# Seven half products for the last outputs of a feed-forward, with a division and a root moved

## The chip, the cores and the metric

The kernel runs on one core of a Trainium2 chip. The time is that of the device for one execution, in microseconds (us), as the median of several runs. The core has five engines that work at once, each through its own queue in order: TensorE (PE: matmuls; PEld: its weight loads), VectorE (DVE), ScalarE (ACT), GpSimd (POOL) and SyncE (SP, which here only issues transfers). SBUF is the working memory, PSUM the memory of eight banks into which TensorE writes.

## The reference

A transformer block with a condition, in float32. x is 4 x 1024 tokens of 512 features; the condition t gives a scale g and an offset b for each norm.

```python
def _tc_rmsnorm(x, t, gw, gb, bw, bb):
    g = (t @ gw.T + gb)[:, None, :]
    b = (t @ bw.T + bb)[:, None, :]
    inv_rms = jax.lax.rsqrt(jnp.mean(x * x, axis=-1, keepdims=True) + EPS)
    return g * x * inv_rms + b

def _attention(x, Wq, Wk, Wv, Wo):          # 16 heads of 32
    attn = jnp.einsum('blhd,bmhd->bhlm', q, k) / scale
    p = jax.nn.softmax(attn, axis=-1)
    o = jnp.einsum('bhlm,bmhd->blhd', p, v).reshape(B, L, D)
    return o @ Wo.T

def _swiglu(x, gate_w, hid_w, out_w):       # 2048 hidden
    return jax.nn.silu(x @ gate_w.T) * (x @ hid_w.T) @ out_w.T

x1 = x + _attention(_tc_rmsnorm(x, t, g1w, g1b, b1w, b1b), Wq, Wk, Wv, Wo)
y = x1 + _swiglu(_tc_rmsnorm(x1, t, g2w, g2b, b2w, b2b), gate_w, hid_w, out_w)
return x + y
```

## The kernel before

Features lie on the 128 partitions, tokens along the rows; the 4096 tokens are 8 blocks of 512 (n). The order of the work on TensorE, VectorE, ScalarE and GpSimd is the order of the program; transfers on SP are placed by the framework.

**The attention** runs in 256 steps g. A step makes the scores of 4 heads for 256 keys and 256 queries (`scores`, four PSUM banks with the tag sc), copies them to SBUF on ScalarE (`keep`, L323), and keeps a running maximum on VectorE (L328, L331). Four steps are one unit j (4 heads, 256 queries), and kind = g % 4 is a step's place in it. Later steps transpose the maximum (mt, L337), reduce it (L343), split it into three bf16 parts (L345 to L348), transpose these (`parts_T`: pt, L353, at the start of kind 1), spread them over the partitions (sp), copy that to shift (L364), add it to the scores (`shifted`, L369), take the exponential (L372) and multiply with v (`weighted`: av, L382). The sum of the exponentials is built by accumulating transfers that GpSimd issues (L396), folded (L404) and summed by TensorE (sum, L414). `inverse` (L422) and `normalize` (L431) are the division of the softmax on VectorE. A block of tokens is 32 steps.

**The feed-forward** of earlier blocks fills TensorE from step 60 (FS) on: two steps work on one pair p = (g - 60) // 2, that is 128 hidden features for 512 tokens, gate and hid together. Their four products of quarters are made as seven half products (Strassen's scheme in Winograd's form) on sums of weights and tokens that are made ahead; in PSUM they are bank a (gate) and bank b (hid): `pair_15`, `take_5`, `add_15`, `pair_26`, `copy_156`, `pair_7`, `sub_5`, `pair_3`, `pair_4`; then `gate_tanh`, `gate` and `hidden` give the tile h[p]. Four pairs later `filler` multiplies a group of four hidden tiles with out_w (`contract`, q = p - 4, into a bank named pc), in four passes of 512 columns, and `take_contract` (L583) adds it to the residual res, which empties the bank. Banks with the tag w are two; a pair's bank a, pc, pt, sp and sum all take them. ow is loaded one contraction ahead.

In an even step with feed-forward VectorE does, in this order: the add of shift, reduction and parts (kind 0), the running maximum, the take of pc, `sub_5`, and then in kind 0 or 2 the division. `in_first` chooses: kind 0 in steps 0, 4, 8, 16 and 20 of each 32, kind 2 in steps 14, 26 and 30.

**The second norm** of blocks 0 to 6 is spread over the steps: squares on ScalarE, mean over the features by TensorE, a copy (`norm_mean`, L157), a transfer of one row to DRAM and back as 128x4 (`compact`, `take`: "few"), `root` (L173, ScalarE's Sqrt with eps as bias), `invert` (L177, VectorE), `put` (SP, to DRAM), `norm_spread` (SP, back to all partitions as totf), `norm_scale` (L199). For block 0 root and invert stand after step e+20, put e+21, spread e+22; for the others e+20, e+21, e+22, e+24. The exponentials and tanh of ScalarE share a table of functions, Sqrt has another.

**After the attention** (from pair 104 to pair 127) only feed-forward is left: each pair's `filler` is split into two halves between the products. After pair 127 the last four contractions stand alone. The scores' banks are not used there.

Of the kernel before, what the change touches and what calls it, by code (L numbers as in the profile page):

```python
# [9 lines left out]

F32 = mybir.dt.float32
BF16 = mybir.dt.bfloat16
AF = mybir.ActivationFunctionType
ALU = mybir.AluOpType
# [10 lines left out]
def tile_cond_transformer_block(  # L25
# [125 lines left out]
    def norm_mean(tag: str, inside: bool):  # L151
        if inside:
            pm = ps_av.tile([P, NB], F32, tag="av", name=f"pm{tag}")
        else:
            pm = ps.tile([P, NB], F32, tag="w", name=f"pm{tag}")
        mm(pm, ones_mean, state[tag], True, True)
        nc.scalar.copy(state[tag], pm)  # L157

    def compact(tag: str, t, rows: int, n: int):

# [3 lines left out]
    def take(tag: str):  # L164

        src = inv_s.pop(tag)
        few = sb.tile([P, src.shape[0] * src.shape[1] // P], F32, tag="few", name=f"few{tag}", bufs=2)
        nc.sync.dma_start(out=few, in_=src.rearrange("h (p c) -> (h p) c", c=few.shape[1]))
        state["few", tag] = few

    def root(tag: str):
        few = state["few", tag]
        nc.scalar.activation(few, few, AF.Sqrt, bias=eps)  # L173

    def invert(tag: str):
        few = state["few", tag]
        nc.vector.reciprocal(few, few)  # L177

    def put(tag: str):
        few = state.pop(("few", tag))  # L180
# [225 lines left out]
    def take_av(j: int):  # L406
        avs[j] = sb.tile([P, HQ], F32, tag="avs", name=f"avs{j}", bufs=2)
        nc.scalar.copy(avs[j], av.pop(j))
# [176 lines left out]
            nc.sync.dma_start(out=out[n][:, d, :], in_=r)  # L585


    NR = NBLK * C * (NB // HQ) * UN
    GB = C * (NB // HQ)
    BS = GB * UN  # L590
# [15 lines left out]
    def after(g, fn, *a):  # L606
        ended.setdefault(g, []).append((fn, a))
# [40 lines left out]
    for n in range(NBLK):  # L648
        g0 = (n + 1) * BS
        pin(g0 + 6, load_res, n)  # L650
        e = g0 if n == 0 else g0 - 4
        go = e + 13 if n < NBLK - 1 else g0 + 8
        for d in range(C):
            first.append((go, None, project_out, (n, d)))
            pin(go - 3 + (d // 2 * 4 if n else 0), load_wo, n, d)
        if n < NBLK - 1:
            tag = f"f{n}"
            after(e + 16, add_res, n)
            for k in range(2):
# [44 lines left out]
    with tc.manual_schedule(  # L704
# [37 lines left out]
        g = 0  # L742
        END = NR + 12
        NP_ = NBLK * NF

        def filler(p: int, tail: bool = False):

# [8 lines left out]
            if q + 1 < NP_:  # L756
                load_ow(q + 1)
            half = FG // 2
            return (
# [14 lines left out]
        while g < END:  # L774
# [40 lines left out]
                keep(g)  # L815
            if kind == 1 and s_on:
                take_av(j_s)
            due = bool(first) and first[0][0] <= g
            if not ffn:
                if x_on:  # L820
# [24 lines left out]
            elif even:  # L845
# [22 lines left out]
            else:  # L868
# [60 lines left out]
        p0 = (END - FS) // 2  # L929
        for p in range(p0, NP_):  # L930
# [81 lines left out]
```

## Time and profile before

| | |
|---|---|
| median of 3 runs | 2449.82 us (2447.05 to 2451.08) |
| the profiled execution | 2455.29 us, of it span 2453.4 us |
| granted clock of TensorE | 0.994 |
| pc (L112), 4096 matmuls of 512 columns | 470.5 us busy |
| L422 RECIPROCAL 128x256, 64 times | 111.6 us, 1744 ns each |
| L583 take of pc, 128 times | 88.2 us, 689 ns each |
| L353 pt, 128 matmuls | 17.6 us |
| ACT_TABLE_LOAD: L372 13, L173 7, L149 5 and single ones | 1283 ns each |
| L396 accumulations issued by GpSimd, 192 | 165.3 us, 9.3 us to landing |
| ow loads, 128 of 256 KB | 3.1 us to landing |

A matmul in float32 is two instructions and each tile of weights is four of 32 columns, so one pass of 128x128 weights over 256 tokens is 8 rows of the trace. A row's duration reaches beyond the start of the next one; how long TensorE takes is read from start to start. A line of the program can be that of a helper: L112 is `mm`, and the tile's name (pa, pb, pc) tells which product it is.

### The profile page before, as it was taken

To read this page: it belongs to the slowest core of one execution; us is meant where nothing else is said; L and a number is where in the kernel's file an instruction comes from. 1 tells how busy PE (TensorE), PEld (TensorE's weight loads), DVE (VectorE), ACT (ScalarE), POOL (GpSimd) and SP (SyncE) were. 2 spreads that over 40 slices of the span, in tenths; PEclk is the share of its full clock that TensorE was granted. 3 is DMA by queue.
4 is the path that set the end of the run, shared out by engine and by line. 5 is a ranking of instruction groups with operands and counts; after the bars stand their busy time and mean duration, and the time that the engine had idled before them with its cause. 6 is when DMAs were issued, how large, how long until landed. Compare 5 with 4: busy or idle time off the path is not lost. (4 is left out here: it accounts for less than half of the span.)

```text
span 2453.4 us, 72677 instructions
## 1 busy us (share of the span) xinstructions
PE 2385.5 (97%) x32553; PEld 1135.9 (46%) x32553; DVE 1940.7 (79%) x2183; ACT 1413.2 (58%) x1495; POOL 172.4 (7%) x207
## 2 busy tenths in 40 slices
PE   8999999999999999999999999999999999999999
PEld 3333334344444544544454544454445445444444
DVE  2688888878799988998899979997999799843332
ACT  3677776765566656665566656665666566512110
POOL 0000000000000000000000000000000000000000
PEclk9999999999999999999999999999999999999999
DMA  6599999988788788889888888898788888853442
GB/s 216 166 304 259 256 258 240 231 202 219 198 205 210 188 226 209 208 207 229 204 200 213 225 197 209 204 230 207 198 207 203 224 200 204 198 165 117 140 131 70
DMA packets 185988, 501.79 MB, mean 205 GB/s; under 512 B 21319, under 2 KB 78663, under 8 KB 158286
## 3 DMA queue, kind: packets, MB, share of 16 engines
q0 software_dynamic: 28656, 208.68, 43.9%
q1 hardware_dynamic: 156734, 288.47, 35.4%
q8 instruction: 256, 4.19, 0.7%
q14 instruction: 54, 0.44, 0.1%
q10 hardware_dynamic: 288, 0.01, 0.0%
HBM read 246.44 MB, written 41.97 MB: 118 GB/s over the span
## 5 line engine op out<-in xcount | busy, mean ns | idle before, releaser
L369 DVE TENSOR_TENSOR raw<-raw,shift 128x2048 f32<-128x2048 f32 (+1 forms) x320 | 588.8, 1857 | 25.6 <-ACT shift L364 25.6
L323 ACT COPY raw<-sc 128x2048 f32<-128x2048 f32 x256 | 479.7, 1874 | 187.4 <-PE sc L316 130.8
L372 ACT ACTIVATE raw<-raw 128x2048 f32<-128x2048 f32 x256 | 490.8, 1917 | 157.1 <-DVE raw L369 154.8
L328 DVE TENSOR_TENSOR rmax<-rmax,raw 128x1024 f32<-128x1024 f32 x384 | 469.5, 1223 | 48.8 <-ACT raw L323 42.2
L112 PE MATMUL pc<-h,ow 128*32 128x512 f32 x4096 | 470.5, 596 | 5.2 <-DMA ow<-in_out_w 4.2
L382 PE MATMUL av<-raw,v 128*32 128x256 f32 x4096 | 271.9, 383 | 35.6 <-ACT raw L372 35.1
L396 POOL DMA_DIRECT2D raw<-raw x192 | 165.3, 861 | 1967.4 <-ACT raw L372 878.9
L316 PE MATMUL sc<-q,k 32*128 32x256 f32 x4096 | 293.3, 400 | 1.0 <-ACT raw L323 1.0
L112 PE MATMUL pa<-x,fa 128*32 128x256 f32 x4096 | 272.5, 384 | 4.1 <-DVE pa L530 4.1
L112 PE MATMUL pa<-sums,fw 128*32 128x256 f32 x4096 | 271.5, 383 | 0.0
L112 PEld LDWEIGHTS pc<-h,ow 128*32 128x32 f32 x4096 | 128.6, 110 | 250.7 <-issue 231.9
L316 PEld LDWEIGHTS sc<-q,k 32*128 32x128 f32 x4096 | 184.9, 184 | 117.4 <-issue 75.8
L112 PE MATMUL pkq<-y,wkq 128*32 128x512 f32 (+1 forms) x1664 | 232.5, 594 | 4.3 <-ACT y L202 4.1
L112 PEld LDWEIGHTS pa<-x,fa 128*32 128x32 f32 x4096 | 124.7, 110 | 119.7 <-DVE pa L530 21.4
L382 PEld LDWEIGHTS av<-raw,v 128*32 128x32 f32 x4096 | 110.4, 109 | 149.4 <-ACT raw L372 66.0
L112 PEld LDWEIGHTS pa<-sums,fw 128*32 128x32 f32 x4096 | 134.4, 111 | 90.0 <-issue 3.4
L583 DVE SCALAR_TENSOR_TENSOR res<-pc,res 128x512 f32<-128x512 f32 x128 | 88.2, 689 | 78.9 <-PE pc L112 76.2
L545 ACT COPY pb<-pa 128x256 f32<-128x256 f32 x128 | 46.1, 360 | 174.4 <-PE pa L112 173.3
L562 ACT ACTIVATE t<-pa 128x512 f32<-128x512 f32 x128 | 78.1, 610 | 109.9 <-PE pa L112 109.6
L112 PE MATMUL pb<-x,fw 128*32 128x256 f32 x2048 | 134.0, 379 | 1.2 <-ACT pb L545 1.2
L112 PE MATMUL pa<-x,fw 128*32 128x256 f32 x2048 | 134.0, 379 | 0.0
L552 DVE TENSOR_TENSOR pb<-pb,p 128x256 f32<-128x256 f32 x128 | 55.0, 430 | 99.8 <-PE pb L112 94.2
(108 smaller groups left out, 2243.7 us busy)
## 6 DMA issues: line engine op xcount, KB each, us to landing
raw<-raw POOLq DMA_DIRECT2D x192, 1024.0 KB, 9.3
fw<-sw SPq DMA_DIRECT2D x128, 512.0 KB, 7.8
fa<-in_gh_w SPq DMA_DIRECT2D x128, 384.0 KB, 6.8
ow<-in_out_w SPq DMA_DIRECT2D x128, 256.0 KB, 3.1
wkq<-in_kq_w SPq DMA_DIRECT2D x32, 512.0 KB, 6.2
v<-vs SPq DMA_DIRECT2D x128, 128.0 KB, 6.6
k<-kqs SPq DMA_DIRECT2D x124, 128.0 KB, 6.5
kqs<-st SPq DMA_DIRECT2D x61, 256.0 KB, 8.3
```

Source lines behind the costliest of these rows:

```text
L112: nc.tensor.matmul(dst[k : k + n, :], w[:, k : k + n], moving, start=start, stop=stop, skip_group_check=seeded)
L316: nc.tensor.matmul(sc[:, i, k, :], keys[rows, k * P : (k + 1) * P], queries[rows, :], start=True, stop=True)
L323: nc.scalar.copy(raw[r].rearrange("p k h q -> p h k q"), state.pop(("sc", r)))
L328: nc.vector.tensor_tensor(rmax[j], rmax[j], raw[r][:, k, :, :], ALU.max)
L369: nc.vector.tensor_tensor(t, t, s.unsqueeze(1).to_broadcast(list(t.shape)), ALU.add)
L372: nc.scalar.activation(raw[r], raw[r], AF.Exp)
L382: nc.tensor.matmul(av[j][i * DH : (i + 1) * DH, :], v[m, u][:, k, i * DH : (i + 1) * DH], raw[r][:, k, i, :], start=(kt == 0), stop=(kt == ...
L396: nc.gpsimd.dma_start(out=acc[j].rearrange("p k h q -> p (k h q)"), in_=raw[r].rearrange("p k h q -> p (k h q)"), accum_op=ALU.add,)
L545: nc.scalar.copy(bank_b[p][:, RIGHT], bank_a[p][:, RIGHT])
L552: nc.vector.tensor_tensor(b[:, LEFT], b[:, RIGHT], fifth.pop(p), ALU.subtract)
L562: nc.scalar.activation(state["t", p], bank_a[p], AF.Tanh, scale=0.5)
L583: nc.vector.scalar_tensor_tensor(r, pp, 0.5, r, ALU.mult, ALU.add)
```

## The change

Three parts.

1. **Outputs.** The contractions of pairs 108 to 127 and the four after the last pair are made as seven half products, too, with two outputs d and four hidden tiles together. The sums of out_w are made once and kept (for each group and two outputs, 16 pieces of 128x128 in a tile with the tag raw, free by then), the sums of the hidden tiles once for each group. The products are made in the four scores' banks, two of which a matmul each opens first (as L541 does for bank b). ow is no longer loaded for them.
2. **Division.** In steps with feed-forward `divide` is called ahead of `evict` (the take of pc), no longer after `sub_5`.
3. **Root.** `norm_mean` adds eps in its copy. `root` and `invert` are replaced by `inverse_root`, an integer first guess on VectorE and four Newton steps on GpSimd, after step e+21; put comes at e+22, spread at e+23 for block 0 and e+24 for the others.

```diff
-        nc.scalar.copy(state[tag], pm)
+        nc.scalar.activation(state[tag], pm, AF.Identity, bias=eps)
...
-    def root(tag: str):
+    def inverse_root(tag: str):
         few = state["few", tag]
-        nc.scalar.activation(few, few, AF.Sqrt, bias=eps)
-    def invert(tag: str):
-        few = state["few", tag]
-        nc.vector.reciprocal(few, few)
+        y, t = (sb.tile(list(few.shape), F32, tag=f"few{i}", name=f"few{i}{tag}") for i in range(2))
+        nc.vector.tensor_scalar(
+            y.bitcast(I32), few.bitcast(I32), 1, 0x3FFFFFFF, ALU.logical_shift_right, ALU.bitwise_xor
+        )
+        nc.gpsimd.tensor_scalar_mul(y, y, 1.35 * 2.0**62)
+        for _ in range(4):
+            nc.gpsimd.tensor_tensor(t, y, y, ALU.mult)
+            nc.gpsimd.tensor_tensor(t, t, few, ALU.mult)
+            nc.gpsimd.tensor_scalar(t, t, -0.5, 1.5, ALU.mult, ALU.add)
+            nc.gpsimd.tensor_tensor(y, y, t, ALU.mult)
+        state["few", tag] = y
...
+    def output_sums(f: int, k: int):
+        w = sb.tile([P, 16, P], F32, tag="raw", name=f"wt{f}_{k}", bufs=RAW)
+        for i in range(2):
+            nc.sync.dma_start(out=w[:, 4 * i : 4 * i + 4, :], in_=out_w[f, 2 * k + i])
+    def output_sums_add(f: int, k: int):
+        nc.vector.tensor_tensor(s1, a21, a22, ALU.add)
+        nc.vector.tensor_tensor(s2, s1, a11, ALU.subtract)
+        nc.vector.tensor_tensor(s3, a11, a21, ALU.subtract)
+        nc.vector.tensor_tensor(s4, a12, s2, ALU.subtract)
+    def hidden_sums(gr: int):
+        t = sb.tile([P, 4, 2, HQ], F32, tag="raw", name=f"ht{gr}", bufs=RAW)
+        for i in range(4):
+            for k in range(2):
...
+                nc.vector.tensor_tensor(t[:, i, k], a, b, ALU.subtract)
+    def output_steps(gr: int, k: int):
...
+        def step_1():
+            times(a[:, 0], a11, left(one), True)
+        def step_5():
+            times(a[:, 1], s1, sums_of(0))
+            p5.append(sb.tile([P, HQ], F32, tag="avs", name=f"o5_{gr}_{k}", bufs=2))
+            nc.scalar.copy(p5[0], a[:, 1])
+            nc.vector.tensor_tensor(a[:, 1], a[:, 0], p5[0], ALU.add)
+        def step_26():
+            times(a[:, 0], a12, left(two))
+            times(a[:, 1], s2, sums_of(1))
+            nc.scalar.copy(b[:, 1], a[:, 1])
+        def step_7():
+            times(b[:, 1], s3, sums_of(2))
+            nc.vector.tensor_tensor(b[:, 0], b[:, 1], p5[0], ALU.subtract)
+        def step_3():
+            times(a[:, 1], s4, right(two))
+            take(0, a)
+        def step_4():
+            times(b[:, 0], a22, sums_of(3))
+            take(1, b)
...
-            after(e + 20, root, tag)
-            after(e + (20 if n == 0 else 21), invert, tag)
-            after(e + (21 if n == 0 else 22), put, tag)
-            after(e + (22 if n == 0 else 24), norm_spread, tag)
+            after(e + 21, inverse_root, tag)
+            after(e + 22, put, tag)
+            after(e + (23 if n == 0 else 24), norm_spread, tag)
...
                 if g < NR:
                     running_max(g, 0)
                     running_max(g, 1)
+                divide()
                 if evict is not None:
                     evict()
                 pair_7(p)
                 sub_5(p)
...
-            if n_on and j_n < direct and kind in (0, 2):
-                at = g - kind
-                in_first = j_n % GB == GB - 1 or (at >= FS and at % BS not in (12, 24, 28))
-                if in_first == (kind == 0):
-                    inverse(j_n)
-                    if j_n != GB:
-                        normalize(j_n)
+            if not ffn:
+                divide()
...
+        state["outs"] = ps_sc.tile([P, HG, 2, HQ], F32, tag="sc", name="outs")
+        for i in (1, 3):
+            nc.tensor.matmul(...)        # one each into banks 1 and 3
+        def last_filler(p: int):
+            gr, i = (p - FG) // FG, p % FG
+            if i % 2 == 0:
+                return (lambda: (one(), five())), two_six, (lambda: None)
+            return (lambda: (seventh(), three())), four, (lambda: None)
...
+            if p < p0 + NF // FG:
+                for k in range(2):
+                    output_sums((seven // FG - 1 + p - p0) % (NF // FG), k)
...
-            one, two, evict = filler(p, True)
+            one, two, evict = filler(p, True) if p < seven else last_filler(p)
...
+            if p0 + 1 < p <= p0 + 1 + NF // FG:
+                for k in range(2):
+                    output_sums_add((seven // FG - 1 + p - p0 - 2) % (NF // FG), k)
+            if p % FG == FG - 1 and p >= seven - 1:
+                hidden_sums(p // FG)
-        for p in range(NP_, NP_ + FG):
-            one, two, evict = filler(p)
-            one()
-            two()
-            evict()
+        one, other = (output_steps(NP_ // FG - 1, k) for k in range(2))
+        one[0]()
+        other[0]()
+        for i in range(1, 6):
+            one[i]()
+            other[i]()
```

`take(d, bank)` in `output_steps` adds the bank to res on VectorE, as `take_contract` did, and stores the result after the last group. seven is 108, p0 is 104.

More of the change, by code (lines that the diff above doesn't have):

```diff
@@ L11 @@
 F32 = mybir.dt.float32
+I32 = mybir.dt.int32
 BF16 = mybir.dt.bfloat16
@@ L166, in take @@
         src = inv_s.pop(tag)
-        few = sb.tile([P, src.shape[0] * src.shape[1] // P], F32, tag="few", name=f"few{tag}", bufs=2)
+        few = sb.tile([P, src.shape[0] * src.shape[1] // P], F32, tag="few", name=f"few{tag}")
         nc.sync.dma_start(out=few, in_=src.rearrange("h (p c) -> (h p) c", c=few.shape[1]))
         state["few", tag] = few
-    def root(tag: str):
+    def inverse_root(tag: str):
         few = state["few", tag]
-        nc.scalar.activation(few, few, AF.Sqrt, bias=eps)
-    def invert(tag: str):
-        few = state["few", tag]
-        nc.vector.reciprocal(few, few)
+        y, t = (sb.tile(list(few.shape), F32, tag=f"few{i}", name=f"few{i}{tag}") for i in range(2))
[9 more added lines that the diff above has]
+        state["few", tag] = y
     def put(tag: str):
@@ L585, in take_contract @@
             nc.sync.dma_start(out=out[n][:, d, :], in_=r)
+    def output_sums(f: int, k: int):
+        w = sb.tile([P, 16, P], F32, tag="raw", name=f"wt{f}_{k}", bufs=RAW)
+        for i in range(2):
+            nc.sync.dma_start(out=w[:, 4 * i : 4 * i + 4, :], in_=out_w[f, 2 * k + i])
+        state["wt", f, k] = w
+    def output_sums_add(f: int, k: int):
+        w = state["wt", f, k]
+        a11, a12, a21, a22, s1, s2, s3, s4 = (w[:, i : i + 2, :] for i in range(0, 16, 2))
+        nc.vector.tensor_tensor(s1, a21, a22, ALU.add)
+        nc.vector.tensor_tensor(s2, s1, a11, ALU.subtract)
+        nc.vector.tensor_tensor(s3, a11, a21, ALU.subtract)
+        nc.vector.tensor_tensor(s4, a12, s2, ALU.subtract)
@@ new lines, in hidden_halves @@
+    def hidden_halves(gr: int, i: int):
+        return [h[gr * FG + 2 * i + k] for k in range(2)]
+    def hidden_sums(gr: int):
+        t = sb.tile([P, 4, 2, HQ], F32, tag="raw", name=f"ht{gr}", bufs=RAW)
+        one, two = hidden_halves(gr, 0), hidden_halves(gr, 1)
+        for i in range(4):
+            for k in range(2):
+                b11, b12, b21, b22 = one[k][:, LEFT], one[k][:, RIGHT], two[k][:, LEFT], two[k][:, RIGHT]
+                a, b = ((b12, b11), (b22, t[:, 0, k]), (b22, b12), (b21, t[:, 1, k]))[i]
+                nc.vector.tensor_tensor(t[:, i, k], a, b, ALU.subtract)
+        state["ht", gr] = t
@@ new lines, in output_steps, with times, left, right @@
+    def output_steps(gr: int, k: int):
+        banks = state["outs"]
+        a, b = banks[:, 2 * k], banks[:, 2 * k + 1]
+        w = state["wt", gr % (NF // FG), k]
+        a11, a12, _, a22, s1, s2, s3, s4 = (w[:, i : i + 2, :] for i in range(0, 16, 2))
+        one, two, t = hidden_halves(gr, 0), hidden_halves(gr, 1), state["ht", gr]
+        p5 = []
+        def times(dst, weights, moving, start: bool = False):
+            for i in range(2):
+                mm(dst, weights[:, i, :], moving[i], start and i == 0, i == 1, True)
+        def left(tiles):
+            return [x[:, LEFT] for x in tiles]
+        def right(tiles):
+            return [x[:, RIGHT] for x in tiles]
+        def sums_of(i):
+            return [t[:, i, 0], t[:, i, 1]]
+        def take(d: int, bank):
+            n, d = gr * FG // NF, 2 * k + d
+            r = res[n][:, d, :]
+            nc.vector.scalar_tensor_tensor(r, bank.rearrange("p a q -> p (a q)"), 0.5, r, ALU.mult, ALU.add)
+            if gr % (NF // FG) == NF // FG - 1:
+                nc.sync.dma_start(out=out[n][:, d, :], in_=r)
+        def step_1():
[18 more added lines that the diff above has]
+            take(1, b)
+        return step_1, step_5, step_26, step_7, step_3, step_4
@@ L744, in tile_cond_transformer_block @@
         NP_ = NBLK * NF
+        seven = ((END - FS) // 2 // FG + 1) * FG
         def filler(p: int, tail: bool = False):
@@ L755, in filler @@
                 pp = ps.tile([P, NB], F32, tag="w", name=f"pc{q}")
-            if q + 1 < NP_:
+            if q + 1 < seven - FG:
                 load_ow(q + 1)
@@ L817, in tile_cond_transformer_block, with divide @@
                 take_av(j_s)
+            def divide():
+                if n_on and j_n < direct and kind in (0, 2):
+                    at = g - kind
+                    in_first = j_n % GB == GB - 1 or (at >= FS and at % BS not in (12, 24, 28))
+                    if in_first == (kind == 0):
+                        inverse(j_n)
+                        if j_n != GB:
+                            normalize(j_n)
             due = bool(first) and first[0][0] <= g
@@ L929, in tile_cond_transformer_block @@
         p0 = (END - FS) // 2
+        state["outs"] = ps_sc.tile([P, HG, 2, HQ], F32, tag="sc", name="outs")
+        for i in (1, 3):
+            nc.tensor.matmul(
+                state["outs"][:, i].rearrange("p a q -> p (a q)"),
+                select[:, 0, :],
+                select.rearrange("p h c -> p (h c)"),
+                start=True,
+                stop=True,
+            )
+        steps = {}
+        def last_filler(p: int):
+            gr, i = (p - FG) // FG, p % FG
+            if i % 2 == 0:
+                steps[gr, i // 2] = output_steps(gr, i // 2)
+            one, five, two_six, seventh, three, four = steps[gr, i // 2]
+            if i % 2 == 0:
+                return (lambda: (one(), five())), two_six, (lambda: None)
+            return (lambda: (seventh(), three())), four, (lambda: None)
         for p in range(p0, NP_):
```

## The prediction

> **What bounds the kernel now.** I read the page's first two parts for the engine that sets the time, then the list of waits for what stops it, then the timeline of single steps. The page first (busy time and share; then tenths of each of 40 slices):
>
> ```profile
> PE 2385.5 (97%) x32553; PEld 1135.9 (46%) x32553; DVE 1940.7 (79%) x2183; ACT 1413.2 (58%) x1495; POOL 172.4 (7%) x207
> PE   8999999999999999999999999999999999999999
> ```
>
> TensorE has no idle slice, at a granted clock of 0.994. So a change counts in two ways only: columns that TensorE no longer streams, and waits of TensorE that appear or go. VectorE is at 79% over the span, but 9 tenths in most slices before the last six: while scores run, it is just behind. The change moves a division in its queue, so I looked at a step of kind 0 and the start of the next (kind 1). VectorE (start us, duration us, instruction):
>
> ```profile
> 996.66 1.22 DVE L331 TENSOR_TENSOR rmax<-raw 128x1024 f32<-128x1024 f32 x1
> 998.28 0.69 DVE L583 SCALAR_TENSOR_TENSOR res<-pc,res 128x512 f32<-128x512 f32 x1 [0.41 <-PE pc L112]
> 999.22 0.43 DVE L552 TENSOR_TENSOR pb<-pb,p 128x256 f32<-128x256 f32 x1 [0.24 <-PE pb L112]
> 999.56 1.74 DVE L422 RECIPROCAL total<-total 128x256 f32<-128x256 f32 x1
> 1001.33 0.42 DVE L431 TENSOR_TENSOR oT<-avs,total 128x256 f32<-128x256 f32 x1
> 1001.68 2.35 DVE L369 TENSOR_TENSOR raw<-raw,shift 128x1024 f32<-128x1024 f32 x2
> ```
>
> TensorE over the same stretch:
>
> ```profile
> 993.55 1.09 PE L337 MATMUL mt<-ident,rmax 128*128 128x128 f32 x8
> 994.57 3.64 PE L112 MATMUL pc<-h,ow 128*32 128x512 f32 x32
> 998.03 1.05 PE L112 MATMUL pb<-x,fw 128*32 128x256 f32 x16
> 999.03 0.27 PE L353 MATMUL pt<-ident_bf,split 128*32 128x128 bf16 x2
> 999.23 1.15 PE L316 MATMUL sc<-q,k 32*128 32x256 f32 x16
> ```
>
> The reader is to see one coincidence: L583, which empties the bank of pc, ends at 998.97, and the transpose pt starts at 999.03. It is no accident. pt needs a bank with tag w; there are two, one holds the gate sums of the running pair, the other pc. In the step around 604 the take ran 7 us late behind a weight load, ended at 603.94, and pt started at 603.99. Everything of TensorE after pt stands behind it in its queue. So in every step of kind 0 the take is on the path already.
>
> **The change part by part.**
>
> *Division ahead of the take.* The reciprocal and the product with avs now stand between the maximum (L331) and L583. From the rows: consecutive VectorE instructions overlap by 0.08, so the reciprocal starts at 997.80; the product 1.77 later (999.56 to 1001.33 above), 999.57; the take 0.35 after that (1001.33 to 1001.68), 999.92; it ends at 1000.61, and pt starts 0.06 later, at 1000.67 instead of 999.03: **1.64 us of TensorE idle**. Only the 0.41 that VectorE waited for pc hides any of it. In steps 0 and 16 of a block the take waited 0.10 only, which gives 1.94, but there VectorE had a backlog of 0.3 that a stalled TensorE lets it work off; I take 1.65 throughout. Where: kind 0 steps 0, 4, 8, 16 and 20 of each 32 from step 64 on, 30 of them, and step 256. Step 64 has no outputs yet, at 68 the take is late anyway; at 256 VectorE waits 1.22 for pc, so 0.9 remains. 28 x 1.65 + 0.9 = **+47.1**. Nothing gives it back: what follows pt (copy mT, sp, shift, scores' copy, exponential) all starts from pt, and VectorE only idles longer before L369.
> In the steps of kind 2 (14, 26, 30) no transpose follows. At 14 VectorE's idle 0.12 and 0.24 (951.23, 952.16) are filled, and the two TensorE gaps that end that chain, 0.28 at 958.90 and 0.20 at 960.17, go: 0.48 x 6 = **-2.9**. At 26 and 30 there is no idle to fill. At 26 the next gate sums find the bank 0.35 late (1045.87 against 1046.2), which the gap of 1.57 at 1051.29 absorbs.
>
> *The second root.* It leaves ScalarE, and with it two table loads in each of 7 blocks. The first (966.00) lies in idle time. The second does not; ScalarE, then TensorE:
>
> ```profile
> 973.10 0.39 ACT L408 COPY avs<-av 128x256 f32<-128x256 f32 x1
> 973.51 1.28 ACT L372 ACT_TABLE_LOAD   x1
> 974.80 1.91 ACT L372 ACTIVATE raw<-raw 128x2048 f32<-128x2048 f32 x1
> ```
>
> ```profile
> 974.22 1.15 PE L316 MATMUL sc<-q,k 32*128 32x256 f32 x16
> 976.76 1.07 PE L382 MATMUL av<-raw,v 128*32 128x256 f32 x16 [1.39 <-ACT raw L372]
> ```
>
> ScalarE goes copy, load, exponential without a pause, and TensorE idles 1.39 for the exponential. Without the load it comes 1.28 earlier and 0.11 is left: 7 x 1.28 = **-9.0**. The Trainium skill ("ScalarE: Activation LUTs", What ACT_TABLE_LOAD costs) adds a drain of about 1380 ns to the 1283 ns of the load, some 2.66 us for each switch; by that the sum would be 18.6, capped by the gap at 9.7. The rows show no drain (0.01 on either side), so the row decides. The mean's copy with a bias costs 0.07 more, in idle time.
>
> In its place VectorE runs one shift where the small reciprocal stood (0.17, no change), and GpSimd 17 dependent instructions on 128x4. Queued behind them on GpSimd is the next accumulation, at 983.50, late enough; on SP the store of the result waits for them, and behind it stand a v load, the read-back into totf and the next output weights ow. In the trace the store went at 979.10, the read-back 2.65 later; an ow load lands in 3.1, an issue takes 0.33. The weights are needed by pc at 994.57. So 15.5 - 2.65 - 0.33 - 3.1 = 9.4 us are free for the 17, or 0.55 each. The nearest rows are GpSimd's own at the start, a fill and a dependent select on 128x128 that follow each other by about 0.25: 17 x 0.25 = 4.2 us, no cost. Against this speaks the Trainium skill ("SBUF — State Buffer", Who interferes with whom): a VectorE instruction with two SBUF inputs and a GpSimd instruction that reads SBUF exclude each other, the later one blocking to the end of the first. From 978.99 VectorE runs 4.6 us of such instructions (L369 2.26, L328 twice 1.22) and again from 984.5; if the 17 get in once per such instruction and four times in each pause of about 1 us, they need some 12 us, an estimate: 2.5 late, in 6 blocks (the first has no ow): +15. No row of before has GpSimd computing beside VectorE. I take **0**, as the GpSimd row has it; a gain is excluded, since nothing waits for the root today (totf is used only around 1013). Far end +15.
>
> *Seven half products.* The stage after the attention is TensorE alone. Its busy time there (us in the window, engines in the order of the page), and the last stretch:
>
> ```profile
> 2247.20:2433.40 186.20, 186.20 (x2840) 92.03 (x2836) 58.88 (x101) 26.15 (x59) 0.00 (x0) 1.00 0.40 121
> ```
>
> ```profile
> 2433.34 15.63 PE L112 MATMUL pc<-h,ow 128*32 128x512 f32 x144
> ```
>
> No gap at all. A pair takes 9.48 (its first gate product starts at 2237.77, 2247.25, 2256.72) and streams 7 x 512 + 4 x 512 = 5632 columns: 1.683 ns each, the same for 256-column and 512-column products. Two outputs of one group of hidden tiles cost 4096 columns; as seven half products 3584. 24 contractions (20 beside pairs 108 to 127, 4 after) save 24 x 256 = 6144 columns: **-10.3**. What comes back:
> - two seeding matmuls of the scores' banks, one such (L541) takes 0.39: +0.6 for both, between 0.4 and 0.8;
> - at pair 108 the first product of differences needs the hidden sums, which stand on VectorE behind the take (to 2248.2) and eight weight sums of pair 107. An addition of 128x256 in SBUF takes 0.42 and follows the last by 0.34 (L480 to L483): 8 x 0.34 + 0.43 after 2248.1 is 2251.3, while TensorE wants it at 2247.25 + 1.72 + 0.86 = 2249.8: +1.4. At later groups no weight sums stand ahead and the sums are in time: the take to about 0.8 after the pair's end, the first sum at 1.2, wanted at 2.6;
> - after the last pair eight hidden sums end about 3.4 after it, so that the first bank's addition comes at 3.9 where TensorE wants the bank at 3.4: +0.5. Otherwise one bank's copy and addition (0.37 + 0.43) lie behind the other's product of 0.86;
> - the last four results leave within 2.5 us instead of 10: 0 to +1 for the last store, +0.5.
> Between odd pairs the cover of the fifth product's addition falls from 1.72 to 0.86. It ends at 2245.81, the next pair would start at 2246.4: still hidden, by 0.5. The weight loads of 1 MB a pair for four pairs fit where the DMA share is 0.40. Sum of this part **-7.3**.
>
> **Sum.** 47.1 - 2.9 - 9.0 + 0 - 7.3 = **+27.9**. It is made on the profiled execution, which took 2455.29 (span 2453.4, the rest around it), 5.5 over the median of the three shown; the differences do not depend on that, so 2449.82 + 28 = **2478**. Its own range, with a stall of 1.35 to 1.95 at each take (36 to 55), the tail between -9 and -5 and the root at -7 to -10, is 2465 to 2492.
>
> **Rivals.**
> 1. *The later take costs nothing, because pt gets its bank otherwise or VectorE reaches that point earlier.* Then -2.9 - 9.0 - 7.3 = -19.2, **2431**. For it: VectorE waits 0.41 and 0.24 around the take today, which the division fills. Against: of its 2.1 us only 0.41 lies before the take, and 603.94 to 603.99 shows pt following it. It decides from a stall under 19.2 / 28.5 = 0.67 us a step.
> 2. *Half of it is absorbed.* If VectorE's earlier finish of the division shortens the later waits for the exponential (35.1 us in all for av), 19 to 25 of the 47 stay, and the result is within 5 us of before: **2452**. Against: the long ones (1.57 at 1051.29) arise in steps 26 and 27, after VectorE has waited for TensorE again.
> 3. *GpSimd is locked out*, +15 more: **2493**. For it the skill's rule; against, the small size of the work, which fits into VectorE's new idle time after each take.
>
> **How the numbers follow.** The forecast 0.62, the first rival 0.15, the second 0.11, the third 0.12. A change under 0.2% (5 us) is about what a measurement of this kernel cannot tell from none. The first rival is faster; the second gives 0.03 faster, 0.05 same, 0.03 slower; the others are slower: 0.18, 0.05, 0.77. The range takes in the second and third and leaves out the first: 2446 to 2503.
>
> **What would show it.** Right: in the steps of kind 1 after a division, pt starts 0.06 after the take and 1.6 later against pb than before; the take ends 2.7 after the maximum instead of 1.1; the table loads fall by 14 and the gap of 1.39 to about 0.1; the last stage shortens by 7, with one gap at pair 108. Wrong: steps 1, 5, 9, 17, 21 of a block no longer than before, or pt waiting for something else. GpSimd's 17 instructions lasting over 9 us, with pc waiting for ow two steps later, would be the third rival.

## The result

The changed kernel takes 2547.36 us (median of 4 runs, 2541.72 to 2547.90), the kernel before in the same series 2450.45 (median of 4; a fourth run, of 3478.25 us, stands beside the three shown above and hardly moves the median): **1.0395 times the time before, 95% interval 1.0374 to 1.0416**. That is 97 us more, where 28 had been forecast. The sign was right, the size was not, and the time lies outside the range. The profiled execution took 2547.13 us (span 2545.3).

The page of the changed kernel, its first two parts, then the row of one of its groups, behind it the same row of before (busy time, mean ns | idle time ahead of it and what ended it):

```profile
PE 2402.1 (94%) x33131; PEld 1155.9 (45%) x33131; DVE 1975.2 (78%) x2287; ACT 1402.1 (55%) x1498; POOL 265.9 (10%) x326
...
PE   8999999999989999999999999999999998999997
...
POOL 0000000200020002000210002000200020000000
...
L113 PE MATMUL pb<-x,fw 128*32 128x256 f32 x2048 | 139.1, 391 | 21.6 <-ACT pb L553 21.6
```

```profile
L112 PE MATMUL pb<-x,fw 128*32 128x256 f32 x2048 | 134.0, 379 | 1.2 <-ACT pb L545 1.2
```

TensorE's share falls from 97% to 94%. Of the 92 us by which the span is longer, TensorE stands idle for 75 (143.2 us of the span against 67.9) and is busy for 17 more (2402.1 against 2385.5), though it has fewer columns to stream. The slices of POOL show a new visitor: seven places, one for each of blocks 0 to 6, where GpSimd computes. And pb waits 21.6 us in all for a copy of ScalarE, where it waited 1.2.

**The division did what was forecast.** VectorE, then TensorE, at step 20 of a block of 32 and the start of step 21 (the same stretch of before was shown with the prediction):

```profile
1006.31 1.22 DVE L339 TENSOR_TENSOR rmax<-raw 128x1024 f32<-128x1024 f32 x1
1007.45 1.75 DVE L430 RECIPROCAL total<-total 128x256 f32<-128x256 f32 x1
1009.23 0.42 DVE L439 TENSOR_TENSOR oT<-avs,total 128x256 f32<-128x256 f32 x1
1009.57 0.69 DVE L591 SCALAR_TENSOR_TENSOR res<-pc,res 128x512 f32<-128x512 f32 x1
```

```profile
1007.69 1.05 PE L113 MATMUL pb<-x,fw 128*32 128x256 f32 x16
1010.31 0.27 PE L361 MATMUL pt<-ident_bf,split 128*32 128x128 bf16 x2 [1.57 <-DVE res L591]
```

The take ends at 1010.26, 2.7 after the maximum ended, and pt starts 0.05 later, behind an idle of 1.57. The view of the tile pt counts such waits:

```profile
  DVE res L591: 48.1, 29
```

48.1 us in 29 places, of which the trace of before has none; the sum in the prediction had 47.1, from 28 and a smaller one. They are not all alike: pt waits 1.57 in steps 5, 9 and 21, but 1.88 in steps 1 and 17:

```profile
1111.93 0.27 PE L361 MATMUL pt<-ident_bf,split 128*32 128x128 bf16 x2 [1.89 <-DVE res L591]
```

The prediction had worked out 1.94 for these steps and then put them down to 1.65.

**The rest was not forecast.** GpSimd in the same block (each row: start, duration, instruction, and in brackets the idle time before it):

```profile
988.82 2.18 POOL L179 TENSOR_SCALAR few0f<-few0f 128x4 f32<-128x4 f32 x1 [9.50 <-DVE few0f L176]
...
993.74 0.20 POOL L184 TENSOR_TENSOR few0f<-few0f,few1f 128x4 f32<-128x4 f32 x1
...
994.29 2.21 POOL L182 TENSOR_TENSOR few1f<-few1f,fewf 128x4 f32<-128x4 f32 x1
...
1003.93 0.20 POOL L184 TENSOR_TENSOR few0f<-few0f,few1f 128x4 f32<-128x4 f32 x1
1004.43 0.91 POOL L404 DMA_DIRECT2D raw<-raw  x1 [0.31 <-issue]
```

The chain lasts from 988.82 to 1004.13, 15.3 us, and the accumulation (L404) that stands behind it in GpSimd's queue goes out at 1004.43. Some 20 us later this reaches ScalarE and, through it, TensorE:

```profile
1026.11 1.87 ACT L331 COPY raw<-sc 128x2048 f32<-128x2048 f32 x1 [7.26 <-DMA raw<-raw]
1027.88 0.38 ACT L553 COPY pb<-pa 128x256 f32<-128x256 f32 x1
```

```profile
1028.31 1.94 PE L113 MATMUL pb<-x,fw 128*32 128x256 f32 x16 [3.94 <-ACT pb L553]
1030.17 2.09 PE L324 MATMUL sc<-q,k 32*128 32x256 f32 x16
```

The next accumulation waits for this one's landing and leaves at 1014.60, some 10 us later, and so on. A late one hands back its buffer of the tag raw late; the copy of the scores waits 7.26 for a buffer; behind it in ScalarE's queue is the copy that pb needs; and TensorE stands still for 3.94. After that the same 16 matmuls last 1.94 where they last 1.05 elsewhere, and the scores 2.09 in place of 1.15. The view by windows (busy time of PE, PEld, DVE, ACT and POOL, then the granted clock, DMA share and GB/s) tells why:

```profile
1023.63:1027.04 3.41, 0.74 (x8) 0.00 (x0) 0.00 (x0) 0.93 (x1) 0.50 (x1) 1.00 0.98 372
1027.04:1030.45 3.41, 2.14 (x20) 0.88 (x24) 2.40 (x3) 3.04 (x3) 0.43 (x2) 0.50 0.91 214
1030.45:1033.87 3.42, 3.42 (x32) 1.73 (x36) 3.42 (x6) 1.54 (x1) 0.78 (x1) 0.50 1.05 207
```

TensorE's clock is halved for two windows of 3.41 us. In the profile of before there are 6 such windows between 592 us and the last matmul, in that of the changed kernel 18: eleven with such a wait of pb in steps 22 and 23, four after the division's wait of 1.88 (below), three elsewhere.

**The stage after the attention grew.** From the mean of the last norm (pmf) to the end of the span before takes 239.6 us, in the changed kernel 249.8: 10.2 more, where -7.3 was forecast. Its columns are fewer as counted; but in every odd pair from 109 on, and in nearly every step after the last pair, a product waits:

```profile
2343.51 1.07 PE L113 MATMUL outs<-h,wt 128*32 128x256 f32 x16 [0.62 <-DVE outs L670]
...
2532.48 1.07 PE L113 MATMUL outs<-ht,wt 128*32 128x256 f32 x16 [0.61 <-DVE outs L670]
2534.11 1.07 PE L113 MATMUL outs<-h,wt 128*32 128x256 f32 x16 [0.56 <-DVE outs L670]
2535.99 1.07 PE L113 MATMUL outs<-h,wt 128*32 128x256 f32 x16 [0.81 <-DVE res L650]
```

The first of these writes the right half of bank a. L670, which it waits for, works in bank b.

### The profile page after: what moved, and what is told of

Its sections match the earlier page's. It is cut to its first block, busy times and chain, and to the rows that moved or that the text cites. A ratio compares the mean times of both kernels' runs of the same rounds, so it can differ in the third digit from the quotient of the medians.

```text
span 2545.3 us, 74065 instructions
## 1 busy us (share of the span) xinstructions
PE 2402.1 (94%) x33131; PEld 1155.9 (45%) x33131; DVE 1975.2 (78%) x2287; ACT 1402.1 (55%) x1498; POOL 265.9 (10%) x326
## 5 line engine op out<-in xcount | busy, mean ns | idle before, releaser
L377 DVE TENSOR_TENSOR raw<-raw,shift 128x2048 f32<-128x2048 f32 (+1 forms) x320 | 589.6, 1858 | 95.2 <-ACT shift L372 95.2
L113 PE MATMUL pc<-h,ow 128*32 128x512 f32 x3328 | 381.6, 598 | 2.9 <-DMA ow<-in_out_w 2.0
L404 POOL DMA_DIRECT2D raw<-raw x192 | 165.6, 862 | 1881.1 <-ACT raw L380 753.4
L324 PE MATMUL sc<-q,k 32*128 32x256 f32 x4096 | 301.7, 409 | 1.2 <-ACT raw L331 1.2
L390 PE MATMUL av<-raw,v 128*32 128x256 f32 x4096 | 279.2, 392 | 23.6 <-ACT raw L380 23.1
L113 PE MATMUL pa<-x,fa 128*32 128x256 f32 x4096 | 269.9, 381 | 4.2 <-DVE pa L538 2.5
L113 PE MATMUL pa<-sums,fw 128*32 128x256 f32 x4096 | 267.8, 379 | 0.0
L113 PE MATMUL pkq<-y,wkq 128*32 128x512 f32 (+1 forms) x1664 | 231.2, 593 | 4.3 <-ACT y L210 4.1
L113 PEld LDWEIGHTS pc<-h,ow 128*32 128x32 f32 x3328 | 103.6, 110 | 209.5 <-issue 195.0
L113 PEld LDWEIGHTS pa<-x,fa 128*32 128x32 f32 x4096 | 123.3, 109 | 113.0 <-DVE pa L538 20.4
L113 PEld LDWEIGHTS pa<-sums,fw 128*32 128x32 f32 x4096 | 132.8, 110 | 88.2
L113 PE MATMUL pb<-x,fw 128*32 128x256 f32 x2048 | 139.1, 391 | 21.6 <-ACT pb L553 21.6
L363 ACT COPY mT<-pt 12x256 bf16<-12x256 bf16 x64 | 23.2, 362 | 223.6 <-PE pt L361 223.6
L113 PE MATMUL pa<-x,fw 128*32 128x256 f32 x2048 | 134.3, 380 | 0.0
L113 PE MATMUL pb<-sums,fa 128*32 128x256 f32 x2048 | 133.9, 379 | 0.0
L113 PEld LDWEIGHTS pkq<-y,wkq 128*32 128x32 f32 (+1 forms) x1664 | 72.8, 117 | 127.7 <-issue 116.7
```

The lines of the kernel that those rows point to most:

```text
L113: nc.tensor.matmul(dst[k : k + n, :], w[:, k : k + n], moving, start=start, stop=stop, skip_group_check=seeded)
L324: nc.tensor.matmul(sc[:, i, k, :], keys[rows, k * P : (k + 1) * P], queries[rows, :], start=True, stop=True)
L363: nc.scalar.copy(mT[j][:NP], pt[:NP, :, :].rearrange("p a b -> p (a b)"))
L377: nc.vector.tensor_tensor(t, t, s.unsqueeze(1).to_broadcast(list(t.shape)), ALU.add)
L390: nc.tensor.matmul(av[j][i * DH : (i + 1) * DH, :], v[m, u][:, k, i * DH : (i + 1) * DH], raw[r][:, k, i, :], start=(kt == 0), stop=(kt == ...
L404: nc.gpsimd.dma_start(out=acc[j].rearrange("p k h q -> p (k h q)"), in_=raw[r].rearrange("p k h q -> p (k h q)"), accum_op=ALU.add,)
```

## The experiments

Ten kernels. "Before" is the median of the runs of before beside them (2448.60, 2449.51 and 2450.31 us in three series).

| kernel | median us | ratio to before (95%) | half-clock windows |
|---|---|---|---|
| division alone | 2497.32 | 1.0202 (1.0175 to 1.0230) | 3 |
| root alone | 2485.55 | 1.0150 (1.0132 to 1.0168) | 11 |
| seven half products alone | 2463.81 | 1.0057 (1.0039 to 1.0074) | 3 |
| the same, a tile for each bank | 2447.13 | 0.9991 (0.9983 to 1.0000) | 2 |
| and its weights loaded later | 2445.19 | 0.9983 (0.9976 to 0.9991) | 4 |
| root on VectorE | 2447.55 | 0.9991 (0.9983 to 1.0000) | 3 |
| root on GpSimd in three lots | 2444.78 | 0.9981 (0.9974 to 0.9988) | 2 |
| division, product twice | 2534.76 | 1.0348 (1.0333 to 1.0362) | 19 |
| that, with scores made twice | 2506.37 | 1.0225 (1.0210 to 1.0240) | 0 |
| best of the parts | 2437.36 | 0.9942 (0.9926 to 0.9957) | 3 |

The last column counts windows of 3.41 us at half clock, from 592 us to the last matmul, in the one profiled execution of each. Another execution can have others: of the four of the division alone, one took 2507.72 us at a clock of 0.993, the profiled one 2497.71 at 0.996.

### One part at a time

The first kernel has only this:

```diff
                 if g < NR:
                     running_max(g, 0)
                     running_max(g, 1)
+                divide()
                 if evict is not None:
                     evict()
```

> The kernel before with the division alone moved ahead of the take. Theory: the waits of pt for the take grow by about 50 us as in the changed kernel's trace, and because TensorE then stands idle for 1.6 us in one window of its clock more often, the granted clock falls for some windows of 3.4 us more, worth 5 to 15 us: 2510 us (2500 to 2520). Rival A: the waits are all of it and the clock has other causes: 2494 us. Rival B: the division costs nothing by itself and the changed kernel's loss comes from late accumulations: 2445 to 2453 us.

Measured: +48.7 us, clock 0.996. Rival A is right: the waits are all of it. The tile pt waits `DVE res L583: 48.1, 29` as in the whole change, and only 3 windows are at half clock. My theory had added 5 to 15 us for the clock; where the border lies, the section on the clock shows.

The second has `norm_mean`, `take`, `inverse_root`, `put` and `norm_spread` of the change and nothing else.

> The kernel before with the second root alone moved to GpSimd. Theory: ScalarE's table loads go (-10 us), but the 17 instructions hold GpSimd's queue for 10 to 15 us, the accumulations behind them start late, the scores' copy waits for a raw buffer at step 22 of each block, and TensorE stands idle there 4 us and runs at half clock for some windows after it: 4 to 6 us for each of six blocks, 2450 - 10 + 30 = 2470 us (2460 to 2482). Rival: the late accumulations only show where the division has made the queue late already, and the root alone gains: 2440 us.

Measured: +37 us, somewhat over the upper end, and nothing of the rival. Fourteen table loads are gone, and step 18 of each of seven blocks is 1.41 us shorter, as in the change, where the product with v no longer waits (it waited 1.39 for the exponential before):

```profile
985.30 1.15 PE L324 MATMUL sc<-q,k 32*128 32x256 f32 x16
986.42 1.07 PE L390 MATMUL av<-raw,v 128*32 128x256 f32 x16
```

The chain takes it back several times over. TensorE in this kernel, one block earlier than the rows above:

```profile
746.33 3.62 PE L113 MATMUL pc<-h,ow 128*32 128x512 f32 x32
754.10 1.94 PE L113 MATMUL pb<-x,fw 128*32 128x256 f32 x16 [4.15 <-ACT pb L553]
755.97 1.79 PE L324 MATMUL sc<-q,k 32*128 32x256 f32 x16
```

The same wait and the same half clock behind it, without the division. Against before, steps 21 to 23 are 6.8 to 8.3 us longer in each of the six blocks that have feed-forward there. Together that is 46.4 us; less 7 x 1.41 for the table loads it is 36.5, which is the +37.

The third has the new functions and the loops after the attention alone.

> The kernel before with the seven half products alone, as they are in the change (one tile of four banks). Theory: the columns saved are -10, and the waits of the products for other banks' work in the same tile about +20: 2460 us (2456 to 2464). Rival: these waits come from VectorE's state that the other two parts left behind, and the part alone gains the 7 us forecast: 2443 us.

Measured: +15.2 us. The rival falls: the waits have nothing to do with the other parts. The three parts alone add up to 48.7 + 37.0 + 15.2 = 100.9 us; together they cost 97. So each can be explained by itself, but for a few us: the half-clock windows fall differently in each kernel.

### Whose bank a product waits for

```diff
-    ps_sc = ctx.enter_context(tc.tile_pool(name="ps_sc", bufs=1, space=PSUM))
...
+    sc_pool = tc.tile_pool(name="ps_sc", bufs=1, space=PSUM)
+    ps_sc = sc_pool.__enter__()
...
-        state["outs"] = ps_sc.tile([P, HG, 2, HQ], F32, tag="sc", name="outs")
+        sc_pool.__exit__(None, None, None)
+        ps_out = ctx.enter_context(tc.tile_pool(name="ps_out", bufs=1, space=PSUM))
+        state["outs"] = [ps_out.tile([P, 2, HQ], F32, tag=f"o{i}", name=f"outs{i}") for i in range(HG)]
...
-        a, b = banks[:, 2 * k], banks[:, 2 * k + 1]
+        a, b = banks[2 * k], banks[2 * k + 1]
```

> As the run before, but with four tiles of one bank each in place of one tile of four banks; products, columns and order of the instructions unchanged. Theory (a product waits for the last access to any part of its tile, so separate tiles take away the waits between banks): 2443 us (2439 to 2447). Rival (the products truly need what they wait for): 2460 us, as with one tile.

Measured: 2447.13 us, at the upper edge of the theory and 13 below the rival; and the profile has the theory's picture. From pmf to the end it takes 232.4 us: 7.2 less than before, and 17.5 less than with one tile. Of the waits of odd pairs none is left, of those after the last pair one; TensorE, in the order of time:

```profile
2430.21 1.07 PE L113 MATMUL outs<-h,wt 128*32 128x256 f32 x16 [0.73 <-DVE outs L654]
2431.10 1.05 PE L113 MATMUL outs<-ht,wt 128*32 128x256 f32 x16
```

So products with one tile waited for work in other parts of it. In these two kernels the framework orders by tile, not by bank: the same products, in four banks and in the same order, wait with one tile and do not with four.

The stage is 7.2 us shorter, the whole kernel 1.5. Where did the rest stay? Just ahead of that stage. In this kernel, and then in before, TensorE at the last sum of exponentials:

```profile
2166.91 0.64 PE L415 MATMUL sum<-raw,ones_sum 128*32 128x256 f32 x8 [4.45 <-DVE raw L405]
2168.03 5.11 PE L113 MATMUL pc<-h,ow 128*32 128x512 f32 x32 [0.48 <-ACT total L420]
```

```profile
2171.74 0.64 PE L414 MATMUL sum<-raw,ones_sum 128*32 128x256 f32 x8 [1.64 <-DVE raw L404]
2172.86 3.64 PE L112 MATMUL pc<-h,ow 128*32 128x512 f32 x32 [0.48 <-ACT total L419]
```

The wait is 2.8 longer, and the same 32 matmuls behind it last 5.11 in place of 3.64: half clock again. The queue of SP shows what may be in the way of the last accumulations: `wt`, the 4 MB of weights for the half products, which VectorE first reads at 2235.95:

```profile
2104.10 8.77 SPq L594 DMA_DIRECT2D wt<-in_out_w  x3
...
2148.24 6.57 SPq L594 DMA_DIRECT2D wt<-in_out_w  x6
```

The framework places SP's transfers, and it sent the first of these 132 us ahead of that read. To test whether they are the cause, they were issued by ScalarE, whose order is that of the program:

```diff
-            nc.sync.dma_start(out=w[:, 4 * i : 4 * i + 4, :], in_=out_w[f, 2 * k + i])
+            nc.scalar.dma_start(out=w[:, 4 * i : 4 * i + 4, :], in_=out_w[f, 2 * k + i])
```

> The seven half products with one tile for each bank, and the 16 loads of out_w for them issued by ScalarE at pairs 104 to 107 in place of SyncE, whose queue sent them 100 to 50 us earlier, beside the last accumulations. Theory (these loads delay the last accumulation by 2.8 us, and TensorE's wait for it then costs a half-clock window, 1.7 us): 2443 us (2440 to 2445), and the wait of the last sum is 2.0 us instead of 4.8. Rival (that wait is chance): 2447 us.

Measured: 2445.19 us, just over the theory. Its ratio to before (0.9976 to 0.9991) overlaps that of the four tiles (0.9983 to 1.0000), so that the time alone does not show a gain over them. The rows do: the long wait is gone (`2167.45 0.64 PE L415 MATMUL sum<-raw,ones_sum 128*32 128x256 f32 x8 [0.50 <-PE pa L113]`), but ScalarE's issues now stand ahead of the copy to pb, where TensorE waits 2.05 at 2228.94, in place of 1.20, and a half-clock window follows. Moving the transfers removed one cost and brought another.

### What the root costs on GpSimd

First without GpSimd: the Newton steps as 14 instructions of VectorE.

```diff
-            nc.gpsimd.tensor_tensor(t, y, y, ALU.mult)
-            nc.gpsimd.tensor_tensor(t, t, few, ALU.mult)
-            nc.gpsimd.tensor_scalar(t, t, -0.5, 1.5, ALU.mult, ALU.add)
-            nc.gpsimd.tensor_tensor(y, y, t, ALU.mult)
+            nc.vector.scalar_tensor_tensor(t, y, -0.5, y, ALU.mult, ALU.mult)
+            nc.vector.tensor_tensor(t, t, few, ALU.mult)
+            nc.vector.scalar_tensor_tensor(y, t, 1.5, y, ALU.add, ALU.mult)
```

> The kernel before with the second root alone moved, its Newton steps on VectorE (14 small instructions) in place of GpSimd's 17. Theory (GpSimd's queue is the loss: accumulations behind the chain start late and raw buffers come free late): the loss of the root alone goes, the table loads' 10 us stay gained, VectorE's 14 instructions cost up to 2 us a block: 2444 us (2438 to 2452), and no wait of pb at step 22. Rival (the loss is the later schedule of the root, put and spread): 2480 to 2488 us, as with GpSimd.

Measured: 2447.55 us, within the theory, and pb has no wait in step 22. The loss belongs to GpSimd, not to the root's later place. (Of the 9.9 us won by the table loads 8.4 go back: steps 19 and 20 are 1.4 us longer in six blocks.) The next kernel keeps all 17 on GpSimd, cuts them into three lots with the queue's accumulations in between, and starts them one step earlier:

```diff
-            after(e + 21, inverse_root, tag)
+            after(e + 20, root_start, tag)
+            after(e + 20, root_rounds, tag, 1, False)
+            after(e + 21, root_rounds, tag, 1, False)
+            after(e + 22, root_rounds, tag, 2, True)
```

> The root alone moved to GpSimd as in the change, but the 17 instructions in three lots, behind the accumulations of three steps, the first a step earlier. Same instructions, same neighbours on VectorE. Theory (an accumulation queued behind the whole chain is the loss): an accumulation waits for a third of the chain at most; at least half of the 37 us goes: 2440 to 2465 us. Rival (it is the shared use of SBUF by GpSimd and VectorE, or the root's later end): 2478 to 2490 us.

Measured: 2444.78 us, 4.7 faster than before, where the uncut chain is 37 slower. GpSimd in the same block as in the rows of the uncut chain:

```profile
709.67 1.12 POOL L178 TENSOR_SCALAR few0f<-few0f 128x4 f32<-128x4 f32 x1 [8.89 <-DVE few0f L175]
...
713.39 1.18 POOL L186 TENSOR_TENSOR few0f<-few0f,few1f 128x4 f32<-128x4 f32 x1
714.51 0.90 POOL L407 DMA_DIRECT2D raw<-raw  x1
...
724.50 1.05 POOL L186 TENSOR_TENSOR few0f<-few0f,few1f 128x4 f32<-128x4 f32 x1
725.49 0.89 POOL L407 DMA_DIRECT2D raw<-raw  x1
```

The 17 are as slow as before, 15.9 us from first to last. But an accumulation goes out between the lots (7 us later than its like at 707.15 with the uncut chain), and the next leaves at 725.49, where with the uncut chain it left at 730.26. Counted from the scores of step 81 in each kernel, the second leaves after 18.5 us in place of 25.2; before, it was 15.3. So the lots make it 3 us late, the whole chain 10, and each accumulation waits for the one ahead: with the lots, the place at which pb waited 4.15 has no wait at all. What costs is the delay of the queue, not the slowness of the instructions as such. The lots also start 5 us earlier than the chain (709.67 against 714.64); no run separates that from the cut.

### What idle time does to the clock

In the traces of before, of the change and of the first four experiments I laid the windows of 3.41 us over TensorE's idle time. Of the windows at full clock between 592 us and the end of TensorE's work, every one with more than 0.55 of it idle was followed by one at half clock; of those with less than 0.5 none; between 0.5 and 0.55 both occurred (so the 1.8 us of the next expectation, 0.53 of a window, is not a sharp border). The six runs after these agree. Two windows of the change show it, at the step after a division:

```profile
1108.96:1112.37 3.41, 1.52 (x26) 0.82 (x22) 3.23 (x5) 0.13 (x1) 0.29 (x1) 1.00 0.54 125
1112.37:1115.78 3.41, 3.41 (x40) 1.86 (x40) 0.46 (x1) 0.82 (x2) 0.57 (x1) 0.50 0.97 231
```

Busy 1.52 of 3.41, and the next window has half clock. A wait of 1.57 us is 0.46 of a window and stays below the border; one of 1.88 is 0.55 and lies on it, if it falls into one window. With the division alone all eleven of these were divided between two windows, so that none cost more than itself: that was luck of the place, and it held in every block, since a block took 266.2 us there, 78 windows. In the change five fell into one window, and four of them brought half clock. By this, 0.42 us more should cost far more than 0.42. The product behind the reciprocal was made twice, in the steps of kind 0 with feed-forward:

```diff
-        nc.vector.tensor_tensor(oT[n, hg][:, qh * HQ : (qh + 1) * HQ], avs.pop(j), total, ALU.mult)
+        for _ in range(2 if ahead else 1):
+            nc.vector.tensor_tensor(oT[n, hg][:, qh * HQ : (qh + 1) * HQ], avs[j], total, ALU.mult)
+        avs.pop(j)
```

> The division alone moved, with the product after it (0.42 us on VectorE) made twice in the 28 steps of kind 0, so that TensorE stands idle 2.05 us ahead of pt instead of 1.63. Theory (in all six traces a clock window of 3.41 us with over 1.8 us of idle is followed by one at half clock, and one with less is not; 1.63 lies below, 2.05 above where it falls into one window, in somewhat over half of the cases): 28 x 0.42 = 12 us of waits and about 16 windows more at half clock, 16 x 1.7 = 27 us: 2497 + 39 = 2536 us (2520 to 2548), granted clock near 0.986. Rival (idle time costs only itself): 2509 us (2506 to 2513), granted clock 0.996.

Measured: 2534.76 us, clock 0.986, 19 windows at half clock where there were 3. The waits of pt grew from 48.1 to 61.4 us; 13 of the 37 us are waiting; the other 24 go with the 16 more windows at half clock, each of which can cost up to 1.7.

Then the reverse: in those steps the scores are made twice, the first time ahead of pt, while TensorE would wait.

```diff
+            fill = kind == 1 and ffn and g < NR and (j_n % GB == GB - 1 or (g - 1) % BS not in (12, 24, 28))
+            if fill:
+                scores(g)
             if kind == 1 and m_on:
                 parts_T(j_m)
             if g < NR:
-                scores(g)
+                scores(g, fill)
```

> The run with the doubled product again, and in the same steps the scores are made once more ahead of pt, into the same banks: 1.07 us more of TensorE work of no use, in the time in which it waits. Theory (a window with over half of it idle brings the half clock): pt still waits for the same take, but only 1.0 us of it is idle, no window is over half idle there, and the 16 or so windows at half clock go: 2535 - 27 = 2508 us (2503 to 2515), granted clock 0.996. Rival (the clock falls for another reason, or the added work delays): 2535 to 2565 us.

Measured: 2506.37 us. TensorE has 30 times 16 matmuls more to do and the kernel is 28 us faster; no window at half clock is left after 592 us. The order at one such step, TensorE:

```profile
1103.74 1.15 PE L316 MATMUL sc<-q,k 32*128 32x256 f32 x16
1106.16 0.27 PE L353 MATMUL pt<-ident_bf,split 128*32 128x128 bf16 x2 [1.27 <-DVE res L585]
1106.36 1.15 PE L316 MATMUL sc<-q,k 32*128 32x256 f32 x16
```

pt still waits for the take; the idle time is merely shorter (31.3 us in all, after 61.4).

### The parts that gain, together

Division as before, the root on GpSimd in three lots, the half products with a tile for each bank, their weights issued by ScalarE at the end of a pair, and this order on VectorE:

```diff
+            if p % FG == FG - 1 and p >= seven - 1:
+                hidden_sums(p // FG)
             if p0 + 1 < p <= p0 + 1 + NF // FG:
                 for k in range(2):
                     output_sums_add((seven // FG - 1 + p - p0 - 2) % (NF // FG), k)
-            if p % FG == FG - 1 and p >= seven - 1:
-                hidden_sums(p // FG)
```

> The version that the runs point to: division as before; root on GpSimd in three lots; seven half products with one tile for each bank, out_w loaded from ScalarE's queue at the end of pairs 104 to 107 (not ahead of the copy that pb waits for), and the hidden sums ahead of the weight sums on VectorE. Theory (the parts add): -4.7 - 4.3, and 1.5 to 3 less for the copy and the half-clock window behind it: 2438 us (2435 to 2442), faster than both. Rival (the parts share a gain, such as a half-clock window that each removes): 2443 to 2446 us.

Measured: 2437.36 us, 0.9942 times before (0.9926 to 0.9957): 13 us faster than before and 110 faster than the change. The wait of 1.49 at pair 108 is gone; a half-clock window at 2223.42, behind the copy to pb, is not.

## Why the prediction was wrong

| step of the prediction | forecast us | the part alone |
|---|---|---|
| division ahead of the take, with the steps of kind 2 | +44.2 | +48.7 |
| root, table loads less, GpSimd at 0 | -9.0 | +37.0 |
| seven half products | -7.3 | +15.2 |
| sum | +27.9 | +100.9 |

- **The division: right** in mechanism and place, and in size by a mean of two errors: 17 waits of 1.57 and 11 of 1.88 for 28 of 1.65 (48.1 us in all against 47.1). Rivals 1 and 2 fall. The 2.9 us to be won in step 14 did not come: steps 14 and 15 last as long as before in all six blocks. That the waits alone cost no half clock was luck (above), and in the whole change it did not hold.
- **The table loads: right.** 1.41 less in step 18 of each of seven blocks, 1.28 forecast; the whole gap went.
- **GpSimd's 17 instructions at 0: the step that failed, by 46 us.** Two things were wrong in it. First the duration. I took the nearest row, 0.25 us each with VectorE idle, over the Trainium skill's rule ("SBUF — State Buffer", Who interferes with whom) that a VectorE instruction with two inputs in SBUF and a GpSimd instruction that reads SBUF exclude each other. The trace sides with the rule: the L182 that starts at 994.29 lasts 2.21 and ends at 996.50, beside an L377 of VectorE (`994.16 2.28 DVE L377 TENSOR_TENSOR raw<-raw,shift 128x2048 f32<-128x2048 f32 x1`) that ends at 996.44. Of the 119 instructions of the seven chains, 67 last 0.19 to 0.35; each of the 52 that last over 1 us ends 0.05 to 0.09 after such an instruction of VectorE. By themselves 17 would take some 4.8 us (they follow each other by 0.28), near the 4.2 of the prediction; the chain came to 15.3, over the 12 that I worked out from the rule and put aside. Second the path. I followed the store on SP to ow and pc, and that wait did not come. I named the accumulation behind the chain, and called it late enough because it was due at 983.50; but the chain shifted what came after it, and I did not follow a raw buffer from there to the scores' copy. So the far end of +15 and rival 3, too, had the lock-out right and the wait wrong.
- **The clock was left out:** I read 0.994 and put it at nothing. Some four tenths of the cost of the late accumulations are the clock behind the wait: at 1028.31 TensorE lost 3.94 us to the wait itself and, in the 5.6 us of the two windows at half clock in which it was busy, half of that, 2.8.
- **The seven half products: columns, seeds (0.38 each) and the wait at pair 108 (1.49, forecast 1.4) right.** With separate tiles the stage shortens by 7.2, forecast 7.3. What failed is the sentence that the fifth product's addition is hidden by 0.5 and that otherwise one bank's work lies behind the other's product. It took for granted that a product waits for its own bank only. With one tile of four banks that cost 17.5 us. And that the weight loads fit by the DMA share was said of the stage in which they are used; they were sent in the stage before, where the last sum then waited 4.45 us in place of 1.64.

Two things stay open. With the loads on SP the last sum waits, with the loads on ScalarE the copy to pb is late, and either brings a half-clock window; a version free of both was not tried. Nor was GpSimd's chain tried away from VectorE's two-input instructions, so that the exclusion itself is seen in the rows and not by a run that removes it.

## What to carry to other kernels

Price an instruction in a queue twice: by its own duration beside the neighbours that it will really have, and by the delay of everything behind it, followed through buffers to the engine that sets the end. Ask of every tile that several engines touch what the framework orders by; here it was the tile, not the bank. And count idle time of TensorE at its own length only while it stays under half of a clock window; in these runs more than that put the next window at half clock, up to 1.7 us more, so that filling a wait, even with useless work, was faster than leaving it empty. Where a wait falls in its window differs from kernel to kernel, so one run without that cost does not show that the wait is free of it.

## What was not expected of the hardware

- TensorE's clock falls to half after a window of 3.41 us that is a little over half idle. The Trainium skill ("TensorE: Matmul & The Clock Gate", Part 1) names the window and the half rate, and an idle window as the cause; here the measurement goes further: 1.9 us of idle time within one were enough (0.55 of 3.41, all windows of six traces), and from half clock 0.37 of a window idle kept it there for another (at 1027.04, busy 2.14 of 3.41, followed by 0.50).
- The windows do not move with the program: starts of half-clock stretches in the changed kernel are 1027.04, 1112.37, 1300.11, 1385.44, 1573.17, 1658.51 us, multiples of 3.413 apart. A later block of that kernel takes 273.0 to 273.1 us, which is 80 windows, so the same steps fell into nearly the same place of a window in block after block.
- GpSimd's instruction on 128x4 takes 0.20 us by itself and 1.0 to 2.2 beside VectorE's two-input instructions: the 52 long ones of the changed kernel all end 0.05 to 0.09 after the one of VectorE.
